# Moving each expert's short tile from last to third of five in a mixture-of-experts kernel, with two-tile transpositions and an earlier count

## The chip, the cores and the metric

The kernel runs on one core of a Trainium2 chip. Its engines are TensorE (PE in the profile; its weight loads are PEld), VectorE (DVE), ScalarE (ACT), GpSimd (POOL) and SyncE (SP). The metric is the device time of one execution in microseconds, lower is better. The core's span is the time from the first to the last instruction of the program in a profiled execution.

## The reference

`x` is 8 x 256 tokens of 1024 values. A gated feed-forward layer with a low-rank correction, chosen per batch, gives `cond`; a router then sends every token to two of eight experts, and the mean of the two experts' outputs is added to `x`.

```python
def cond_layer(x):                              # F = 2752, rank 16
    gate = x @ W_gate.T + 0.5 * (x @ A_gate[i].T) @ B_gate[i].T
    up   = x @ W_up.T   + 0.5 * (x @ A_up[i].T)   @ B_up[i].T
    act  = silu(gate) * up
    return act @ W_down.T + 0.5 * (act @ A_down[i].T) @ B_down[i].T

def experts(c):                                 # E = 8, TOP_K = 2, D = H = 1024
    logits = c @ W_gate + b_gate
    _, top = top_k(logits, 2)
    y_all = relu(einsum('bsd,edh->bseh', c, W_e) + b_e)
    return take_along_axis(y_all, top[..., None], axis=2).mean(axis=2)

out = x + experts(cond_layer(x))
```

All of it is in float32.

## The kernel before

The first 1600 us compute `cond` with Strassen's scheme in two halves of 1024 tokens, write its rows to DRAM (`cond_rows`) and work out the routing. The change does not touch that part.

The rest handles the experts. 4096 token rows go to 8 experts, about 512 to each, and are cut into tiles of 128 rows. An expert has `NJ` = 5 tile positions, 40 in all (`NPOS`). Tiles 0 to 3 of an expert are nearly always full; tile 4 holds what exceeds 512 rows, so it has few rows or none. Expert 0 is shifted by one, because one of its tiles is done ahead (`pre_tile`, L1259): its position 3 is the short one, and its position `NJ - 1` is a leftover tile that is empty in this run. Here four short tiles are empty (the leftover and position 3 of expert 0, experts 1 and 6), and five have at most 32 rows (experts 2, 3, 4, 5 and 7). Five positions of expert 0 and of experts 1 to 7 are 40; 31 of them are full tiles.

A tile goes through these steps:

- `load_rows` (L1437) gathers the tile's 128 rows of `cond_rows` with an indirect DMA on POOL's queue, `AHEAD` = 4 tiles ahead in `SEQ`.
- `rows_transposed` (L1124) transposes them: two halves of four TensorE transposes each, each half in a PSUM bank of its own (`ps_g`), copied out by ScalarE (L1133). Four sums of these blocks (`s`) follow on VectorE, or on POOL for expert 0's two short tiles.
- `one_tile` (L1497) claims four PSUM banks (`tile_banks`, L1208) and branches on the row count (L1501, L1508, L1511): more than 64 rows take `whole` (Strassen, L1153: 28 products, 56 matmul records, 14 pairs that run side by side in two halves of the array, each pair 0.86 us), 33 to 64 and 1 to 32 take `plain` (L1459) with fewer rows, and none takes `empty_tile`, which only writes 64 KB to spare rows. All engines go through the branches. `add_rows` (L1211) adds the result's rows to `out` with an indirect DMA on POOL's queue.
- In `strassen`, the first product in bank `px` is read by VectorE (`u`, L1188) before the eleventh pair may add to that bank; `py`, `pz`, `pw` and then `px` are evicted at the end (L1190 to L1199), each whole tile ending with `z<-z,v`.

PSUM has 8 banks, all from the pool of L89. The planner of the framework hands them out: a whole or a short tile takes four, a transposed tile two.

The order of the tiles is `SEQ` (L1526). `BEHIND` (L1529 to L1533) lists which tiles are transposed behind which: behind tile 0 of an expert its tile 2, behind tile 1 its tile 3, behind tile 2 the next expert's tile 0 and its own tile 4, behind tile 4 the next expert's tile 1. The weights of the next expert are loaded on SP's queue in tile 0's place (four loads of 1 MB, L1091), and the four sums of weight blocks (`ws`, L1103, `sums_e`) run on VectorE behind tiles 1 (two), 2 and 3, the sum of biases (L1205, L1206) behind tile 3. The framework's planner keeps the order of each engine's instructions close to the order in which the program writes them, with what isn't ready by its own reckoning put later; everything inside a branch is one unit that nothing is mixed into.

After the last tile `over`, `ntile`, `novf` and `nov` (L1601 to L1613) count the tiles beyond five per expert (none here), `value` (L1487) loads the count into a register on every engine, and L1615 branches on it.

Of the kernel before, what the change touches and what calls it, by code (L numbers as in the profile page):

```python
# [9 lines left out]
I32 = mybir.dt.int32  # L10
# [3 lines left out]
ALU = mybir.AluOpType  # L14
AX = mybir.AxisListType
P = 128
# [4 lines left out]
E, TOP_K = 8, 2  # L21
T = B * S
# [24 lines left out]
C_THR = C_END + E  # L47
# [6 lines left out]
NJ = 5  # L54
NPOS = E * NJ
# [10 lines left out]
def tile_lora_glu_then_moe(ctx: ExitStack, tc: tile.TileContext, a: dict, out: bass.AP):  # L66
# [11 lines left out]
    nc = tc.nc  # L78

    const = ctx.enter_context(tc.tile_pool(name="const", bufs=1))  # L80
# [10 lines left out]
    def behind(ins, others):  # L91

        for o in others:
            tc.add_manual_dep(
                ins.ins,
                o.ins.name,
                mybir.DependencyInfo(mybir.DependencyClass.NoSync, mybir.DependencyReason.DATA),
                reason="this goes first",
            )
# [4 lines left out]
    add, sub = ALU.add, ALU.subtract  # L104
# [94 lines left out]
    ctab = const.tile([P, C_ALL], F32, name="ctab")  # L199
# [61 lines left out]
    def load_lora_gu(h):  # L261
        lora[h, "raw"] = lp.tile([P, H], F32, tag="raw", name=f"raw_gu{h}")
        return gather(lora[h, "raw"], a["A_gu"], rows["gu", h])
# [615 lines left out]
    cnt = const.tile([P, 2, E], F32, name="cnt")  # L879
# [3 lines left out]
    def small(shape, name, dt=F32, tag=None):  # L883
        return const.tile(shape, dt, tag=tag or name, name=name)
# [195 lines left out]
    def load_e(e, first=()):  # L1080

        m = e % 2
        if m == 0 and W[0] is None:
            W[0] = {
                (kh, nh): xp.tile([P, WB], F32, tag=f"x1_{kh}{nh}", name=f"we_{kh}{nh}")
                for nh in range(2)
                for kh in range(2)
            }
            WS[0] = [xp.tile([P, WB], F32, tag=f"xt1_{i}", name=f"ws_{i}") for i in (1, 2, 3)]
        loads = [  # L1090
            nc.sync.dma_start(W[m][kh, nh], a[f"W_e{kh}{nh}"][e * P : (e + 1) * P, :])  # L1091
            for kh, nh in ((0, 0), (0, 1), (1, 1), (1, 0))
        ]
        for ins in loads:
            behind(ins, first)
        return loads

    def sums_e(e, which, first=()):
        b11, b12, b21, b22 = (W[e % 2][kh, nh] for kh in range(2) for nh in range(2))
        t = WS[e % 2]  # L1100
        for i in which:
            x, y = ((b12, b11), (b22, t[0]), (b22, b12), (b21, t[1]))[i]
            ins = nc.vector.tensor_tensor(t[i], x, y, sub)  # L1103
            behind(ins, first)
            if e == 1:
                issued.append(ins)
# [3 lines left out]
    adds, earlier = [], []  # L1110
# [92 lines left out]
    def sum_bias(dst, b, first=()):  # L1203
        b0, b1 = b[:, :NB], b[:, NB:]
        behind(nc.vector.tensor_copy(dst[lo], b0[lo]), first)  # L1205
        behind(nc.vector.tensor_tensor(dst[hi], b0[hi], b1[hi], sub), first)  # L1206
# [75 lines left out]
    ins = load_lora_gu(0)  # L1282
# [21 lines left out]
    for h in range(2):  # L1304
# [8 lines left out]
        if h == 0:  # L1313
            first = [latest["v"]]
# [30 lines left out]
    for n, (h, g) in enumerate(steps):  # L1345
# [4 lines left out]
        for i in range(NI):  # L1350
            if n and out_rows:

                lo_, hi_, at = out_rows.pop(0)
                ins = nc.gpsimd.dma_start(out[at : at + hi_ - lo_, :], a["x"][lo_:hi_, :])
# [77 lines left out]
    def load_bias(e):  # L1432
        nc.sync.dma_start(braw[e % 2], a["b_e"][e : e + 1, :].partition_broadcast(P))
# [3 lines left out]
    def load_rows(i, col):  # L1437
        gathered[i] = gp.tile([P, H], F32, tag="g", name=f"g{i}")
        issued.append(indirect(gathered[i], cond_rows, col))
# [47 lines left out]
    def value(table, i):  # L1487
        return nc.values_load(  # L1488
            table[:1, i : i + 1], skip_runtime_bounds_check_because="worked out on VectorE"
        )  # L1490
# [6 lines left out]
    def one_tile(i, n, at, gT, A):  # L1497

        m, col = i // NJ % 2, columns(i)[1]
        done, banks = [], tile_banks(i)  # L1500
        with tc.If(n > at + HALF) as full:  # L1501
            done.append(add_rows(whole(i, A, m, banks), P, col))
        if at < 0:
            with full.Else():
                done.append(empty_tile(i))
            return done
        with full.Else():
            with tc.If(n > at + HALF // 2) as half:  # L1508
                done.append(add_rows(plain(i, gT, m, 2, banks), HALF, col))
            with half.Else():  # L1510
                with tc.If(n > at) as some:  # L1511
                    done.append(add_rows(plain(i, gT, m, 4, banks), HALF // 2, col))
                with some.Else():
                    done.append(empty_tile(i))
        return done

    def columns(i):


        if i == NJ - 1:  # L1520
            return gidx1, sidx1
        c = i + 1 if i < NJ else i
        return gidx[:, c : c + 1], sidx[:, c : c + 1]


    SEQ = [0, 1, NJ - 1] + list(range(2, NJ - 1)) + list(range(NJ, NPOS))  # L1526


    BEHIND = {0: (NJ - 1, 2), 1: (3,), NJ - 1: (NJ,), 2: (NJ + 1,), 3: ()}  # L1529
    late = []  # L1530
    for i in range(NJ, NPOS):
        j = i % NJ
        BEHIND[i] = ((i + 2,), (i + 2,), (i + 3, i + 2), (), (i + 2,))[j]  # L1533
    AHEAD = 4
    for i in SEQ[:3]:
        load_rows(i, columns(i)[0])
    load_bias(0)
    first = list(issued)
# [3 lines left out]
    for e in range(E):  # L1542
        n = value(cnti, e)
        for j in range(NJ):
            i = SEQ[e * NJ + j]
            if j + e == 0:
                load_rows(SEQ[3], columns(SEQ[3])[0])
            if e * NJ + j + AHEAD < NPOS:
                k = SEQ[e * NJ + j + AHEAD]
                load_rows(k, columns(k)[0])  # L1550
            if i == NJ - 1:
                tile_done = one_tile(i, value(cnti, E), -HALF, *ready.pop(i))
            else:
                tile_done = one_tile(i, n, (i % NJ + (e == 0)) * P, *ready.pop(i))
            adds += tile_done
            issued.clear()
            if e == 0 and j == 4:
                sums_e(1, (1, 3), tile_done)
                sum_bias(bsum[1], braw[1], tile_done)
            while late:  # L1560
                late.pop()()
            if e + 1 < E:

                if j == 0:
                    for ins in load_e(e + 1):
                        if e == 0:
                            for row in first:
                                tc.add_manual_dep(
                                    ins.ins,
                                    row.ins.name,  # L1570
                                    mybir.DependencyInfo(
                                        mybir.DependencyClass.Sync, mybir.DependencyReason.DATA
                                    ),
                                    reason="rows first",
                                )
                            issued.append(ins)
                    load_bias(e + 1)
                elif e:
                    sums_e(e + 1, ((), (0, 2), (1,), (3,), ())[j], tile_done)
            for k in BEHIND[i]:  # L1580
                if k < NPOS:
                    short = k in (3, NJ - 1)
                    ready[k] = transposed(
                        k, op=pop if short else vop, late=late if k == NJ + 1 else None
                    )
            if e == 0 and j == 2:
                sums_e(1, (0, 2), tile_done)
            if 0 < e < E - 1 and j == 3:
                sum_bias(bsum[(e + 1) % 2], braw[(e + 1) % 2], tile_done)
        earlier[:] = adds  # L1590
        adds.clear()


    NTT = T // P
    op = ctx.enter_context(tc.tile_pool(name="over", bufs=1))

    def osmall(shape, name, dt=F32):
        return op.tile(shape, dt, tag=name, name=name)

    over = osmall([P, E, NTT], "over")  # L1600
    ins = nc.vector.tensor_tensor(  # L1601
        over,
        cnt[:, 1].unsqueeze(2).to_broadcast([P, E, NTT]),
        ctab[:, C_THR : C_THR + NTT].unsqueeze(1).to_broadcast([P, E, NTT]),
        ALU.is_gt,
    )
    behind(ins, earlier)
    ntile = osmall([P, E], "ntile")
    nc.vector.tensor_reduce(ntile, over, AX.X, add)
    novf = osmall([P, 1], "novf")  # L1610
    nc.vector.tensor_reduce(novf, ntile, AX.X, add)
    nov = const.tile([P, 1], I32, name="nov")
    nc.vector.tensor_copy(nov, novf)  # L1613
    nover = value(nov, 0)
    with tc.If(nover > 0):  # L1615
        before = osmall([P, E, E], "before")
        vop(
# [219 lines left out]
```

## Time and profile before

| | us |
|---|---|
| median of 3 runs | 2098.92 |
| lowest and highest run | 2092.86, 2099.81 |
| the profiled execution's own time | 2096.54 |
| its span, first to last instruction | 2094.7 |
| TensorE busy | 2052.9 (98%) |
| VectorE busy | 1246.9 (60%) |
| GpSimd busy | 1057.9 (51%) |
| ScalarE busy | 250.4 (12%) |
| mean granted TensorE clock | 0.995 of full speed |

Rows of the timeline give start and duration in us, engine, line, operation, names of the tiles written and read, shapes, and in brackets how long the engine was idle before and what ended that. `PEq`, `DVEq` and the like are the engines' sequencers, which run branches, register loads and waits. A row of the windows view gives a stretch of time, its length, each engine's busy time and number of instructions, the granted clock, and the share and rate of the DMA engines.

The experts' stage in us from the span's start: the tile done ahead until 1613, expert 0 from 1616.7, experts 1 to 7 from 1664.2, 1723.3, 1785.2, 1847.3, 1907.3, 1968.6 and 2026.9; the last tile's matmuls end at 2084.1.

### The profile page before, as it was taken

Reading aid. Unit: us, or ns where it says so; the run is one execution under the profiler, and the core shown is the slowest. Engines: PE = TensorE matmul, PEld = TensorE weight load, DVE = VectorE, ACT = ScalarE, POOL = GpSimd, SP = SyncE. Lnnn points to the kernel's source line nnn. Section 1 sums busy time; section 2 is a strip of 40 time slices with the busy share of each in tenths; the row PEclk is TensorE's granted clock in tenths of the full one; section 3 lists DMA queues with packets and bytes.
Section 4 is the critical chain, followed back from the end, with each engine's and each line's share of the span. In section 5 each row is a group of like instructions: output and inputs, shape, how many; then the busy total and the mean of one; then the engine's idle time right before and its main releaser. Section 6 shows DMA issues by size and latency. Waiting matters only on the chain. (4 is left out here: it accounts for less than half of the span.)

```text
span 2094.7 us, 20377 instructions
## 1 busy us (share of the span) xinstructions
PE 2052.9 (98%) x6864; PEld 867.2 (41%) x6864; DVE 1246.9 (60%) x1734; ACT 250.4 (12%) x450; POOL 1057.9 (51%) x976
## 2 busy tenths in 40 slices
PE   8999999999999999999999999999999999999997
PEld 3444444444444444444444444444444433333332
DVE  6757466565656656566545443654556676666674
ACT  1001011110101011110100001100002111212111
POOL 2447676675667757665355553565542432322221
PEclk9999999999999999999999999999999999999999
DMA  7675676757667575686433335222324754565632
GB/s 313 246 263 191 241 254 217 261 174 271 209 228 292 182 260 192 230 286 200 144 125 126 126 118 176 101 95 87 118 83 157 222 160 133 159 181 166 182 75 46
DMA packets 108234, 381.73 MB, mean 182 GB/s; under 512 B 12656, under 2 KB 21136, under 8 KB 100304
## 3 DMA queue, kind: packets, MB, share of 16 engines
q1 hardware_dynamic: 81280, 297.98, 40.2%
q0 software_dynamic: 13952, 58.53, 10.6%
q10 hardware_dynamic: 12848, 23.22, 3.1%
q8 instruction: 90, 1.47, 0.3%
q14 instruction: 64, 0.52, 0.1%
HBM read 318.47 MB, written 72.74 MB: 187 GB/s over the span
## 5 line engine op out<-in xcount | busy, mean ns | idle before, releaser
L335 PE MATMUL ps_u<-x,wi 128*128 128x512 f32 x880 | 396.1, 593 | 0.5 <-DMA x<-in_xq 0.5
L113 POOL TENSOR_TENSOR cond<-cond,u_d 128x512 f32<-128x512 f32 x120 | 150.2, 1267 | 231.5 <-DVE u_d L108 231.5
L335 PEld LDWEIGHTS ps_u<-x,wi 128*128 128x128 f32 x880 | 166.9, 190 | 212.4 <-issue 202.0
L335 PE MATMUL ps_u<-x,w 128*128 128x512 f32 x520 | 241.7, 599 | 0.3 <-DMA x<-xs 0.2
L1215 POOL DMA_INDIRECT out<-y,sidx x36 | 74.9, 2080 | 325.8 <-ACT y L1122 295.5
L1174 PE MATMUL ps_x<-we,gT 128*64 128x512 f32 x496 | 231.7, 611 | 1.7 <-DVE z L108 1.1
L108 DVE TENSOR_TENSOR u_u<-ps_u,u_u 128x512 f32<-128x512 f32 x210 | 144.9, 690 | 141.1 <-PE ps_u L335 135.6
L108 DVE TENSOR_TENSOR cond<-ps_d,cond 128x512 f32<-128x512 f32 x160 | 103.8, 686 | 115.2 <-POOL cond L113 40.8
L1174 PE MATMUL ps_z<-ws,s 128*64 128x512 f32 x372 | 157.7, 592 | 0.0
L335 PEld LDWEIGHTS ps_u<-x,w 128*128 128x128 f32 x520 | 96.0, 190 | 134.0 <-issue 126.5
L335 PE MATMUL ps_d<-a,wd 128*128 128x512 f32 x320 | 151.3, 595 | 0.0
L108 DVE TENSOR_TENSOR u_d<-ps_d,u_d 128x512 f32<-128x512 f32 x120 | 82.9, 691 | 113.5 <-PE ps_d L335 111.5
L335 PE MATMUL ps_d<-at,wd 128*128 128x512 f32 x320 | 150.4, 592 | 0.0
L335 PE MATMUL ps_d<-at,wds 128*128 128x512 f32 x320 | 145.1, 596 | 0.0
L1174 PE MATMUL ps_y<-ws,s 128*64 128x512 f32 x248 | 119.8, 628 | 0.0
L113 POOL TENSOR_TENSOR acc<-acc,u_u 128x512 f32<-128x512 f32 x60 | 74.3, 1267 | 86.3 <-DVE u_u L108 74.2
L335 PE MATMUL ps_u<-xt,wi 128*128 128x512 f32 x240 | 112.8, 592 | 0.0
L1174 PE MATMUL ps_x<-ws,gT 128*64 128x512 f32 x248 | 111.5, 592 | 0.0
L1174 PE MATMUL ps_y<-we,s 128*64 128x512 f32 x248 | 111.5, 592 | 0.0
L1174 PEld LDWEIGHTS ps_x<-we,gT 128*64 128x64 f32 x496 | 66.2, 140 | 103.7 <-issue 102.9
L108 DVE TENSOR_TENSOR u<-ps_z,u 64x512 f32<-64x512 f32 x62 | 42.6, 687 | 103.0 <-PE ps_w L1174 85.8
L113 POOL TENSOR_TENSOR wi<-w 128x256 f32<-128x256 f32 x100 | 85.4, 874 | 26.3 <-PE ps_u L335 18.3
(273 smaller groups left out, 3135.2 us busy)
## 6 DMA issues: line engine op xcount, KB each, us to landing
x<-xs SPq DMA_DIRECT2D x240, 512.0 KB, 4.6
x<-in_xq SPq DMA_DIRECT2D x74, 512.0 KB, 4.8
we<-in_W_e SPq DMA_DIRECT2D x32, 1024.0 KB, 10.2
a<-act SPq DMA_DIRECT2D x42, 512.0 KB, 4.7
w<-in_W SPq DMA_DIRECT2D x20, 1024.0 KB, 9.2
wd<-in_W_d SPq DMA_DIRECT2D x40, 512.0 KB, 3.2
xs<-xi SPq DMA_DIRECT2D x24, 512.0 KB, 2.9
out<-in_x POOLq DMA_DIRECT2D x22, 512.0 KB, 4.0
```

The source lines that it names most:

```text
L108: ins = nc.vector.tensor_tensor(dst, x, y, op)
L113: ins = nc.gpsimd.tensor_tensor(dst, x, y, op)
L335: ins = nc.tensor.matmul(ps, A(ai, j), X(xi, j), start=(j == 0 and bank is None), stop=(j == n - 1 and stop), skip_group_check=True,)
L1174: ins = nc.tensor.matmul(dst, w[:, k, :], x[:, k * NB : (k + 1) * NB], start=start, stop=stop, skip_group_check=True,)
L1215: added = nc.gpsimd.indirect_dma_start(out=out, out_offset=bass.IndirectOffsetOnAxis(ap=col[:n], axis=0), in_=y[:n], in_offset=None, compu ...
```

## The change

Four things change.

- `SEQ` puts position 4 third for every expert, as it was for expert 0 alone: 0, 1, 4, 2, 3.
- `BEHIND` follows. Behind the first tile of an expert the third and fourth in the new order are transposed (tile 4 and tile 2), behind the second the fifth (tile 3), behind the fourth (tile 2) the first two tiles of the next expert (tiles 0 and 1), and behind tile 4 and the fifth nothing. Expert 0's leftover tile no longer has a transposition behind it; the next expert's first two tiles are both transposed behind its tile 2.
- The sums of weight blocks move with it: two behind the third place (the short tile, index `j` = 2) and two behind the fourth (tile 2), none behind the second. The sum of biases stays at index 3, which is now tile 2.
- The count of further tiles and its load into registers move from the end of the program to just behind expert 7's tile 1, before the transposition there; the branch on it stays at the end.

```diff
-    SEQ = [0, 1, NJ - 1] + list(range(2, NJ - 1)) + list(range(NJ, NPOS))
+    SEQ = [e * NJ + j for e in range(E) for j in (0, 1, NJ - 1, *range(2, NJ - 1))]

-    BEHIND = {0: (NJ - 1, 2), 1: (3,), NJ - 1: (NJ,), 2: (NJ + 1,), 3: ()}
+    BEHIND = {0: (NJ - 1, 2), 1: (3,), NJ - 1: (), 2: (NJ, NJ + 1), 3: ()}
+    for n in range(NJ, NPOS):
+        j = n % NJ
+        ahead_ = ((2, 3), (4,), (), (5, 6), ())[j]
+        BEHIND[SEQ[n]] = [SEQ[n - j + m] for m in ahead_ if n - j + m < NPOS]
     late = []
-    for i in range(NJ, NPOS):
-        j = i % NJ
-        BEHIND[i] = ((i + 2,), (i + 2,), (i + 3, i + 2), (), (i + 2,))[j]
+    NTT = T // P
+
+    def tiles_over(first):
+        over = small([P, E, NTT], "over")
+        ins = nc.vector.tensor_tensor(
+            over,
+            cnt[:, 1].unsqueeze(2).to_broadcast([P, E, NTT]),
+            ctab[:, C_THR : C_THR + NTT].unsqueeze(1).to_broadcast([P, E, NTT]),
+            ALU.is_gt,
+        )
+        behind(ins, first)
+        ntile, novf, nov = small([P, E], "ntile"), small([P, 1], "novf"), small([P, 1], "nov", I32)
+        nc.vector.tensor_reduce(ntile, over, AX.X, add)
+        nc.vector.tensor_reduce(novf, ntile, AX.X, add)
+        nc.vector.tensor_copy(nov, novf)
+        return ntile, value(nov, 0)
...
                 elif e:
-                    sums_e(e + 1, ((), (0, 2), (1,), (3,), ())[j], tile_done)
+                    sums_e(e + 1, ((), (), (0, 2), (1, 3), ())[j], tile_done)
+            if (e, j) == (E - 1, 1):
+                ntile, nover = tiles_over(tile_done)
             for k in BEHIND[i]:
...
-    over = osmall([P, E, NTT], "over")
...
-    nover = value(nov, 0)
     with tc.If(nover > 0):
```

More of the change, by code (lines that the diff above doesn't have):

```diff
@@ L1591, in tile_lora_glu_then_moe @@
         adds.clear()
-    NTT = T // P
     op = ctx.enter_context(tc.tile_pool(name="over", bufs=1))
@@ L1598, in osmall @@
         return op.tile(shape, dt, tag=name, name=name)
-    over = osmall([P, E, NTT], "over")
[L1601 to L1613, printed above, removed]
-    nover = value(nov, 0)
     with tc.If(nover > 0):
```

## The prediction

> I forecast **2106 us, slower by about 0.35%**. An expert's tiles 0 to 3 are called whole; tile 4 is the short one, which runs few rows or is empty.
>
> **What bounds the kernel now.** First the page, for the bound.
>
> ```profile
> PE 2052.9 (98%) x6864; PEld 867.2 (41%) x6864; DVE 1246.9 (60%) x1734; ACT 250.4 (12%) x450; POOL 1057.9 (51%) x976
> ```
>
> TensorE is busy 98% of the span, so a change is worth what it does to TensorE's idle stretches. The change touches only the experts' tiles, from about 1613 us on. There TensorE's timeline around the first empty short tile (expert 1) reads:
>
> ```profile
> 1717.57 1.02 PE L1174 MATMUL ps_x<-ws,gT 128*64 128x512 f32 x2
> 1720.14 0.63 PE L1130 MATMUL ps_g<-ident,g 128*128 128x128 f32 x4 [1.56 <-DVE z L108]
> 1722.57 0.63 PE L1130 MATMUL ps_g<-ident,g 128*128 128x128 f32 x4 [1.80 <-DVEq L1511]
> ```
>
> Brackets give the idle time before a row and who ended it. The next transposition needs two PSUM banks. Tile 3 and the short tile have claimed four each of the eight (L1208, whether used or not). Its first half waits until VectorE has emptied tile 3, its second until VectorE has left the short tile (L1511). Where the short tile has rows, only the second half waits (expert 2):
>
> ```profile
> 1784.39 0.63 PE L1130 MATMUL ps_g<-ident,g 128*128 128x128 f32 x4 [1.57 <-DVE z L108]
> ```
>
> Now expert 2's two transpositions in a row, behind tile 2:
>
> ```profile
> 1763.58 1.97 PE L1130 MATMUL ps_g<-ident,g 128*128 128x128 f32 x16
> ...
> 1764.53 0.69 DVE L108 TENSOR_TENSOR z<-z,v 64x512 f32<-64x512 f32 x1
> ...
> 1765.47 1.07 PE L1174 MATMUL ps_x<-we,gT 128*64 128x512 f32 x2
> 1765.79 1.54 ACT L1133 COPY gT<-ps_g 128x512 f32<-128x512 f32 x3
> ...
> 1766.41 0.13 PEld L1174 LDWEIGHTS ps_y<-ws,s 128*64 128x64 f32 x1 [0.75 <-ACT gT L1133]
> ```
>
> Here tile 2 and four halves claim all eight banks, and the next tile's second product (ps_y) starts 0.94 us behind its first, when ScalarE's first copy has freed a bank. The other whole tiles last 12.2 us to the next transposition; this one lasts 13.17. Last, expert 0, whose empty tile stands third already:
>
> ```profile
> 1643.87 1.09 PE L1130 MATMUL ps_g<-ident,g 128*128 128x128 f32 x8
> ...
> 1647.07 1.09 PE L1130 MATMUL ps_g<-ident,g 128*128 128x128 f32 x8 [2.11 <-ACTq L1501]
> ```
>
> It is the nearest picture of what every expert becomes.
>
> **The change part by part.** "+" is slower.
>
> *The short tile leaves the end.* Idle time removed: expert 1 3.36, expert 6 3.35, experts 2 to 5 1.57 each (6.28), and ahead of the short tiles 0.29 (expert 3) and 1.09 (expert 5): 14.4 us. The clock record also has 3.41 us at half speed from 1723.7, 1785.1 and 2027.5, behind the short tiles of experts 1, 2 and 6; each costs half of that, together 5.1. The windows view shows the first:
>
> ```profile
> 1718.00:1728.00 10.00, 6.52 (x24) 2.61 (x24) 6.40 (x10) 2.44 (x4) 4.49 (x3) 0.83 0.83 270
> ```
>
> Granted clock 0.83 is 3.41 of 10 us at half speed. The Trainium skill (TensorE: Matmul & The Clock Gate, "Why this matters for your kernels") lets the clock fall only for idle gaps above about 3 us. No gap here reaches that; by the rule nothing is gained, by the row 5.1. I take the row: about 1.8 us of idleness inside one 3.41 us window was enough. Sum -19.5.
>
> *Two transpositions behind tile 0.* Tile 0 now follows tile 3 directly, so those two hold all eight banks. By the rows of 1720.14 and 1722.57 the first half takes a bank of the older tile (free) and the second one of the tile just ended. VectorE's last row of a whole tile ends 1.65 us after its matmuls (1765.22 against 1763.58); the second half could start at 0.55, so 1.1 is lost, 1.2 with the restart. Bounds: 0, if other banks come first, and 1.2; near the upper, because the 0.94 of the other pair lies there. Seven experts, +8.4. Behind tile 2, which follows the short tile directly, the same wait takes the place of 0.94: +0.26 for six, +1.6.
>
> *The short tile third.* With rows it follows a transposition and has old banks. But TensorE must branch past the code of the whole tile, and some branches are slow:
>
> ```profile
> L1501 PEldq COMPARE_BRANCH  x71: 65/184/5422, 1616.4 to 2076.3; - x71
> ```
>
> Seven of the eight short tiles with a full choice of branches meet one of 1.7 to 5.4 us. The Trainium skill (Runtime: NRT & Kernel Launch, "Instruction fetch mechanics") says that a taken branch to code outside the fetched pages waits for a DMA; it speaks against this move. By itself it would charge the whole stall, 3.7 on the average of those seven. By the trace only what exceeds the lead of TensorE's sequencer is lost: 4.9 us ahead at the end of tile 3 (1835.5 against 1840.4), where 4.63 cost 0.29; behind a single transposition it is 3.7 ahead (1687.7 against 1691.4). With stalls of the same sizes the mean loss is 0.73, bounds 0 and 2.3. Experts 2 to 5: +2.9. The rule alone would make it +13.
>
> Empty (experts 1 and 6): tile 2's first bank is one that ScalarE's copy behind tile 1 must free, as in expert 0: 2.1, lower bound 1.10 (expert 0's second empty tile). The clock then falls with a chance of 0.6, 1.0 on average. +6.2.
>
> *Expert 0.* The third place keeps its 2.1. Tile 2's matmuls now fill the rest of that clock window; the 1.7 of the drop at 1648.6 becomes 1.0. One more transposition's sums (four of 0.42) go ahead of the two weight sums before the next tile, whose first eviction was 0.8 late already: +0.8. With +0.3 at the pair: +0.4.
>
> *Count of further tiles.* The chain moves ahead of expert 7's short tile. Its end today:
>
> ```profile
> 2086.10 0.29 DVE L1601 TENSOR_TENSOR over<-cnt,ctab 128x128 f32<-128x128 f32 x1
> ...
> 2086.79 1.32 POOL L1215 DMA_INDIRECT out<-y,sidx  x1 [2.37 <-ACT y L1122]
> 2086.95 0.15 DVE L1613 CAST nov<-novf 128x1 int32<-128x1 f32 x1
> ```
>
> Four VectorE operations take 1.0, five register loads about 0.3 each in parallel. Today they cost nothing: the last rows land at 2090.6, and the end waits for that. Moved, TensorE's load waits for VectorE: 1.65 for tile 1's eviction, 1.0 and 0.36, so 3.0 after tile 1. Behind it are queued the branches and then the short tile's matmuls, which could start at 1.1 and now start about 4.1. The lead is gone, so a slow branch (3.5 in this place today) shows in full, and the clock may fall. Bounds: 0 if the planner puts the load behind the short tile, and 8. I take 5.5, nearest to the chain with a stall.
>
> *The end.* A whole tile now ends the program. Its rows need 5.95 us from issue to the last packet (2069.68 to 2075.63), 32 rows 3.8 (2086.79 to 2090.6); evictions are equal. +1.95. Tile 3 of expert 7 follows tile 2 with no transposition between, and may wait for it up to 1.65: +0.8.
>
> *At nothing.* The weight sums (2.29 each) move to places three and four. From expert 2 on, two of them already run behind tile 2 with eight row sums and end before the next tile needs its first eviction; if three gathered there, VectorE would be 1.5 late per expert. A possible bias sum (1.1) behind them: +0.3. Gathers stay four places ahead on POOL's queue, one issue of 1.0 each; the tightest, behind tile 1's add, lands about 11 us after tile 1 and is needed after 15. SP's weight loads start at tile 3's end and have 27 us.
>
> Sum: -19.5 + 8.4 + 1.6 + 2.9 + 6.2 + 0.4 + 5.5 + 1.95 + 0.8 + 0.3 = +8.6. The profiled execution took 2096.5 (span 2094.7 and 1.8 around it): 2105.1. The runs' median, 2098.9, stands 2.4 higher, as one or two more clock drops would; I add half: **2106**.
>
> **Rivals.** *The count waits for nobody:* its load lands behind the short tile. For it: loads follow the planner's order; against: the chain is written first. -5.5: 2100.5, within 0.3% of the median. *The pairs find free banks:* no second-half waits (10.0): 2096, no change. For it: four banks of tile 3 are long empty; against: the 1722.57 row. *Banks rotate past every conflict:* one mechanism with the sign turned. Besides those 10.0, the 0.94 of the old pairs (6.6) and the idle times of the two empty tiles with their clock (4 of 6.2) go as well, because all pairs take banks emptied a tile ago: about 2085. It decides from about 13 us of the 21. *VectorE collects three weight sums behind tile 2:* 1.5 for six experts, 2115; against: the loads land early.
>
> **How the numbers follow.** Forecast 0.45, count hidden 0.20, free banks 0.18, all banks 0.12, VectorE 0.05. Slower by over 0.3% (about what a measurement of this kernel can tell from no change, 6.3 us) 0.50, within 0.38, faster 0.12. The range 2093 to 2115 leaves out the faster case and some of the last; the forecast alone spans 2101 to 2111.
>
> **What would show it.** Right: no gap ahead of an expert's first tile; behind tile 0, four transposes, a gap near 1.1 that VectorE ends, then twelve; gaps near 2.1 behind tile 1 in experts 1 and 6; in expert 7 TensorE idle 3 us or more behind tile 1. Wrong: tile 0's pair running in 1.97 without a gap and the next tile in 12.2, or the count's load standing behind the short tile.

## The result, and the profile after

The changed kernel takes **2100.18 us** (median of 14 runs, 2096.74 to 2103.1); the kernel before took 2096.73 on the same chip (14 runs). The ratio is 1.0016 with a 95% interval of 1.0009 to 1.0022: slower by 0.16%, less than the 0.3% that I had set as the bound of a change. The forecast was 2106, slower by 0.35%. The profiled execution has a span of 2098.6 us and took 2100.4; against the 2096.5 of before that is 3.9 more, where my sum had 8.6.

TensorE's line of the page answers to the first one shown of before.

```profile
PE 2046.8 (98%) x6864; PEld 858.8 (41%) x6864; DVE 1243.5 (59%) x1734; ACT 250.0 (12%) x450; POOL 1052.0 (50%) x976
```

It is 6 us less busy in a span 4 us longer. The clock record has three half-speed stretches in the stage in place of four, and what was a wait inside a busy row before (the 0.94 of ps_y, while ps_x ran on) is now idle time. Where TensorE stood still, its timeline shows (start, duration, line, operation, in brackets the idle time before it and who ended it). The first three rows are expert 0, the next five expert 3, the last two expert 7.

```profile
1661.71 0.66 PE L1130 MATMUL ps_g<-ident,g 128*128 128x128 f32 x4
1663.57 1.50 PE L1130 MATMUL ps_g<-ident,g 128*128 128x128 f32 x12 [1.21 <-DVE z L108]
1668.91 0.61 PE L1174 MATMUL ps_x<-we,gT 128*64 128x512 f32 x1 [3.83 <-issue]
...
1800.84 0.66 PE L1130 MATMUL ps_g<-ident,g 128*128 128x128 f32 x4
1802.71 1.50 PE L1130 MATMUL ps_g<-ident,g 128*128 128x128 f32 x12 [1.21 <-DVE z L108]
...
1833.09 1.09 PE L1130 MATMUL ps_g<-ident,g 128*128 128x128 f32 x8
1835.06 1.06 PE L1130 MATMUL ps_g<-ident,g 128*128 128x128 f32 x8 [0.88 <-DVE z L108]
...
1845.21 0.64 PE L1174 MATMUL ps_x<-we,gT 128*64 128x512 f32 x1 [0.34 <-DVE u L108]
...
2056.57 1.09 PE L1130 MATMUL ps_g<-ident,g 128*128 128x128 f32 x8
2057.60 0.64 PE L1473 MATMUL ps_x<-we,gT 128*32 128x256 f32 x8
```

1802.71 is what the forecast described: four transposes behind tile 0, a wait of 1.21 us that VectorE ends, then twelve. 1835.06 is the wait in the pair behind tile 2, and 1845.21 a second one inside the tile that follows, which I had not put on the path. 1668.91 is the largest loss of the stage, behind expert 0's second empty place. 2057.60 is what did *not* happen: expert 7's short tile starts at the end of the transposition, although the count had been put in between. The register loads of the count, by line, tell why:

```profile
L1488 SPq TENSOR_LOAD <-nov x1: 273/273/273, 2059.3 to 2059.3; - x1
L1488 PEldq TENSOR_LOAD <-nov x1: 312/312/312, 2081.2 to 2081.2; - x1
L1488 DVEq TENSOR_LOAD <-nov x1: 315/315/315, 2086.6 to 2086.6; - x1
```

SyncE loads the count at 2059.3, behind expert 7's tile 1. TensorE's load stands at 2081.2, behind the branches of the last tile: the planner put it where the value is used.

A ledger of the stage, from the starts of tiles and transpositions in both traces. An undisturbed whole tile takes 12.17 us to the next start, one transposition 1.02, a pair 1.90, a short tile 3.59; what exceeds that is loss. "+" is slower.

| step of the forecast | forecast | measured |
|---|---|---|
| short tile leaves the end (idle time and half clock of before) | -19.5 | -21.8 |
| pair behind tile 0 (six of 1.40, and 0.82 in expert 1's tile 1) | +8.4 | +9.2 |
| pair behind tile 2 (1.53 for 0.93 before, six times) | +1.6 | +3.6 |
| short tile third, with rows | +2.9 | 0 |
| short tile third, empty (2.18; 2.30 and 1.70 of clock) | +6.2 | +6.2 |
| expert 0 up to and with expert 1's tile 0 (12.6 for 7.3) | +0.4 | +5.3 |
| count of further tiles | +5.5 | 0 |
| the end | +1.95 | +2.5 |
| expert 7's tile 3, directly behind tile 2 | +0.8 | -0.2 |
| weight and bias sums | +0.3 | in the third row |
| fewer seams (a pair for two singles, tiles in direct succession) | none | -1.3 |
| the untouched part before 1614.5 | none | +0.5 |
| sum | +8.6 | +4.0 (span +3.9) |

### The profile page after: what moved, and what is told of

Its sections match the earlier page's. It is cut to its first block, busy times and chain, and to the rows that moved or that the text cites. A ratio compares the mean times of both kernels' runs of the same rounds, so it can differ in the third digit from the quotient of the medians.

```text
span 2098.6 us, 20373 instructions
## 1 busy us (share of the span) xinstructions
PE 2046.8 (98%) x6864; PEld 858.8 (41%) x6864; DVE 1243.5 (59%) x1734; ACT 250.0 (12%) x450; POOL 1052.0 (50%) x976
## 3 DMA queue, kind: packets, MB, share of 16 engines
q0 software_dynamic: 13952, 58.53, 10.8%
## 5 line engine op out<-in xcount | busy, mean ns | idle before, releaser
L1174 PE MATMUL ps_z<-ws,s 128*64 128x512 f32 x372 | 162.2, 592 | 0.0
```

The source lines that it names most:

```text
L1174: ins = nc.tensor.matmul(dst, w[:, k, :], x[:, k * NB : (k + 1) * NB], start=start, stop=stop, skip_group_check=True,)
```

## The experiments

Each ratio is against runs of the kernel before on the same chip, taken together with it; "above" or "below the changed kernel" means the difference from its ratio of 1.0016. Each ratio is known to between 0.001 and 0.002 either way, so a difference of about 0.12% between two of them is at the edge of what can be told.

**The count alone.** The kernel before, with only the count moved.

```diff
+            if (e, j) == (E - 1, 1):
+                ntile, nover = tiles_over(tile_done)
             for k in BEHIND[i]:
...
-    over = osmall([P, E, NTT], "over")
...
-    nover = value(nov, 0)
     with tc.If(nover > 0):
```

> The kernel before with one part of the change: the count of further tiles and its register loads stand behind expert 7's tile 1; order, transpositions and weight sums are the old ones. The prediction's step (TensorE's load waits for VectorE behind tile 1 and what is queued behind it stands still): TensorE idle about 3 us behind expert 7's tile 1, time 3 to 5.5 us above the kernel before. The rival (the planner puts TensorE's load where its value is used, at the end): no idle stretch behind that tile, time within 1 us of the kernel before, TensorE's load in the last two tiles.

Measured: 2095.46 us, ratio 0.9996 (0.9985 to 1.0006). Behind expert 7's tile 1 there is no idle stretch, and TensorE's load is again far down, behind the branches of the last tile:

```profile
L1488 SPq TENSOR_LOAD <-nov x1: 272/272/272, 2054.8 to 2054.8; - x1
L1488 PEldq TENSOR_LOAD <-nov x1: 313/313/313, 2080.9 to 2080.9; - x1
```

Moving the count costs nothing and brings nothing. The step of 5.5 us falls.

**The count where every engine must have it.** Was the price wrong, or only the place? A branch that is not taken uses the value at once.

```diff
                 ntile, nover = tiles_over(tile_done)
+                with tc.If(nover > 0):
+                    ordered(nc.gpsimd.dma_start(out[T : T + P, :P], ident))
```

> The changed kernel with a branch on the count right behind its load in expert 7 (not taken here; its body would write 64 KB to spare rows), so that every engine must have the value before it goes on to the short tile. It measures the price that the prediction put on the count. By the prediction: TensorE idle about 3 us or a little more behind expert 7's tile 1, perhaps a half-speed stretch and a slow branch, 5 us above the changed kernel (4 to 8). Rival (the value is ready early enough, the transposition hides it): under 1.5 us of idle time there and no change in time.

Measured: 2104.09 us, ratio 1.0039 (1.0025 to 1.0053), 0.23% or 4.8 us above the changed kernel. TensorE's timeline, VectorE's, the load and a windows row (length, busy times, then granted clock, DMA share and rate):

```profile
2055.22 1.09 PE L1130 MATMUL ps_g<-ident,g 128*128 128x128 f32 x8
2059.43 5.35 PE L1473 MATMUL ps_x<-we,gT 128*32 128x256 f32 x64 [3.12 <-DVE s L108]
```

```profile
2057.75 0.15 DVE L1550 CAST nov<-novf 128x1 int32<-128x1 f32 x1
```

```profile
L1488 PEldq TENSOR_LOAD <-nov x1: 316/316/316, 2057.9 to 2057.9; - x1
```

```profile
2058.00:2068.00 10.00, 8.57 (x80) 4.51 (x82) 3.38 (x8) 2.15 (x6) 2.08 (x2) 0.83 0.36 55
```

The count is done 1.6 us after the transposition's end, the load follows at once, the short tile starts after 3.1 us of idleness and takes 5.35 us in place of 3.66, because the clock fell (0.83 of full speed in that window). 3.1 and 1.7 are the 4.8, and in the profiles the stretch from this transposition to the last matmul is 33.7 us for 28.9. The row names VectorE's `s` sums, which the short tile does not read; TensorE's sequencer goes through the load and five branches, none above 0.24 us, until 2059.3. So the wait on record was right and the 5.5 near, but made up otherwise: a half-speed stretch came, a slow branch did not. The price belongs to a use of the value in that place, which the change doesn't have.

**Expert 0's transpositions as before.**

```diff
-    BEHIND = {0: (NJ - 1, 2), 1: (3,), NJ - 1: (), 2: (NJ, NJ + 1), 3: ()}
+    BEHIND = {0: (NJ - 1, 2), 1: (3,), NJ - 1: (NJ,), 2: (NJ + 1,), 3: ()}
```

> The changed kernel with expert 0's transpositions where they were before (one tile behind its empty third place, one behind its tile 2); the rest as changed. Theory (behind tile 2 the pair's second tile holds TensorE's sequencer at a wait for VectorE, so that the branches of the empty tile behind it start 1.2 us before the work runs out instead of 3, and their 3.4 us show): the gap of 3.83 us ahead of expert 1's tile 0 falls to about 1.1, the half-speed stretch behind it and the pair's 1.21 go, so expert 0 takes 47.5 us from its tile 0 to expert 1's in place of 51.4 and the time falls by 3 to 4 us. Rival (a branch to that code costs its 2.7 us wherever the transpositions stand): the gap stays at 3 us or more and the time within 1.5 us of the changed kernel.

Measured: 2096.69 us, ratio 1.0001 (0.9991 to 1.0011), 0.15% or 3.1 us below the changed kernel. Expert 0 takes 47.35 us from its tile 0 to expert 1's, for 51.44. TensorE's timeline there, and the slow branch (count, shortest/median/longest in ns, start) in this kernel:

```profile
1662.34 1.09 PE L1130 MATMUL ps_g<-ident,g 128*128 128x128 f32 x8
1664.43 0.61 PE L1174 MATMUL ps_x<-we,gT 128*64 128x512 f32 x1 [1.00 <-DVE z L108]
```

```profile
L1511 PEldq COMPARE_BRANCH  x1: 2967/2967/2967, 1660.5 to 1660.5; - x1
```

and the same branch in the changed kernel:

```profile
L1511 PEldq COMPARE_BRANCH  x1: 2718/2718/2718, 1664.4 to 1664.4; - x1
```

The branch is slow in both, 2.97 and 2.72 us. TensorE's sequencer works ahead of the engine, and a branch costs nothing as long as that lead covers it. In the old arrangement it starts at 1660.5, before the last transposition begins (1662.34), and is over by its end. In the new one the transposition's second half waits for VectorE until 1663.57, the branches queued behind that wait run from 1663.6, and the slow one from 1664.4; TensorE is out of work at 1665.08, the register load behind the branch ends at 1668.6, and 3.83 us are lost. A wait in the work took the cover from a branch. In this profile part of the gain is hidden: the branches of expert 1's empty tile were slower than in the changed kernel's profile (3.7 and 3.2 for 2.1 and 2.9) and cost 2.5 us more with the clock.

**Weight sums as before.**

```diff
-                    sums_e(e + 1, ((), (), (0, 2), (1, 3), ())[j], tile_done)
+                    sums_e(e + 1, ((), (0, 2), (1,), (3,), ())[j], tile_done)
```

> The changed kernel with the four weight sums where they were (two behind tile 1, one behind the short tile, one behind tile 2); the rest as changed. Theory (three weight sums of 2.29 us stand in a row behind tile 2 and make VectorE late for tile 3's first eviction): the gaps of 0.34 us inside tile 3 go, tile 3 takes 12.1 to 12.2 us to the next tile in place of 12.63, the gap of 0.88 in the pair ahead of it stays; six experts, 2 to 3 us below the changed kernel. Rival (the row sums or the pair's late copies are what makes VectorE late, or the planner gathers the sums again): 12.6 us and no change in time.

Measured: 2096.06 us, ratio 1.0004 (0.9994 to 1.0014), 0.12% or 2.5 us below the changed kernel, which the times alone can hardly tell; the timeline can. VectorE in the changed kernel, between the end of expert 3's tile 2 and the first eviction of its tile 3:

```profile
1834.12 0.69 DVE L108 TENSOR_TENSOR z<-z,v 64x512 f32<-64x512 f32 x1
1834.84 2.29 DVE L1103 TENSOR_TENSOR ws<-we,we 128x2048 f32<-128x2048 f32 x1
1837.05 2.28 DVE L1103 TENSOR_TENSOR ws<-we,ws 128x2048 f32<-128x2048 f32 x1
...
1839.59 2.28 DVE L1103 TENSOR_TENSOR ws<-we,ws 128x2048 f32<-128x2048 f32 x1
...
1844.47 0.68 DVE L108 TENSOR_TENSOR u<-ps_x,b 64x512 f32<-64x512 f32 x1
```

Three weight sums stand in a row; with eight row sums and a part of the bias sum they keep VectorE busy until 1844.47, when TensorE already waits. With the old arrangement the pair keeps its 0.88 and the tile behind it runs without the second wait:

```profile
1830.38 1.06 PE L1130 MATMUL ps_g<-ident,g 128*128 128x128 f32 x8 [0.88 <-DVE z L108]
```

The tile takes 12.07 us to the next start, for 12.63. So the smallest rival of the forecast ("VectorE collects three weight sums behind tile 2") did come about, at a third of its price: 0.5 per expert, not 1.5.

**Banks handed out by hand.** The compiled program of the changed kernel says which banks are used around the beginning of expert 2 (x, y, z, w are the four banks of a tile, x is emptied last):

```text
expert 1 tile 3:           x7 y1 z4 w0
expert 2 tile 0:           x3 y2 z6 w5
pair behind it, 4 halves:  7 3 0 1
```

The second half gets bank 3, x of the tile just ended, while 0 and 1 have long been free and are given to the third and fourth. Expert 1's tile 0 has x7 y3 z6 w4, and the halves behind it got 0, 5, 1 and 2, none of its banks; there the pair ran without a gap:

```profile
1682.91 1.97 PE L1130 MATMUL ps_g<-ident,g 128*128 128x128 f32 x16
```

The forecast had read the wait as "those two hold all eight banks". The run with named banks tells the two apart: it closes the pool at the start of the experts' part and opens one in which every bank is named.

```diff
+    cps.close()
+    fixed["pool"] = ctx.enter_context(tc.tile_pool(name="psf", bufs=1, space=PSUM))
...
     def tile_banks(i):
-        return [psum(f"ps_{n}{i}") for n in "xyzw"]
+        m = SEQ.index(i) % 2 if fixed else 0
+        return [psum(f"ps_{n}{i}", f"{n}{m}") for n in "xyzw"]
...
+            m = (e * NJ + j + 1) % 2
+            fixed["half"] = [f"{r}{n}" for n in ((m, 1 - m) if len(BEHIND[i]) > 1 else (1 - m,)) for r in "zw"]
             for k in BEHIND[i]:
```

> The changed kernel with its PSUM banks handed out by hand in the experts' part: tiles take two sets of four in turn, and a transposed half takes a bank of a tile's third or fourth product, never of its first two. Theory (the wait of 1.21 us behind tile 0 comes from the choice of the bank that the tile just ended empties last, while three banks of the older tile are free): no gap in the pair behind tile 0 (seven of 1.21), none in the pair behind tile 2, and the gaps of 2.1 us at the three empty third places fall to 1 or less. VectorE's three weight sums behind tile 2 start when that tile's eviction ends, so the 0.88 us saved in that pair come back as waits for tile 3's first eviction (about 1.3 us there). Sum: 8.5 for the first pairs, 4 for the empty places, 2 to 3 for clock: 12 to 15 us below the changed kernel. Rival (all eight banks are taken, so some wait is there whichever bank is chosen): gaps near 1 us stay behind tile 0 and the time within 4 us of the changed kernel.

Measured: 2085.19 us, ratio 0.9951 (0.9933 to 0.9968), 13.6 us below the changed kernel. TensorE, expert 3:

```profile
1796.19 1.97 PE L1134 MATMUL ps_g<-ident,g 128*128 128x128 f32 x16
...
1827.21 1.97 PE L1134 MATMUL ps_g<-ident,g 128*128 128x128 f32 x16
1839.32 0.64 PE L1178 MATMUL ps_x<-we,gT 128*64 128x512 f32 x1 [1.41 <-DVE u L112]
```

Both pairs run in 1.97 without a gap, so nothing needed to wait there. (The change of pools has its price: 3.35 us of idleness ahead of the stage's first transposition, for 1.53.) And as expected, the 0.88 saved in the second pair came back as a longer wait for VectorE, 1.41 for 0.34, since VectorE's three weight sums start no earlier. One step missed: of the three empty third places, expert 0's and expert 6's fell to 0.70 and 0.81 us as expected, but expert 1's rose to 2.89. And behind expert 0 a third transposition came ahead of expert 1's tile 0, with waits of 1.87 and 1.33 us between the three.

**The old order with the same banks.** If all that the short tile cost at the end was a bad bank too, the move would have been needless. The diff is the one above on the kernel before, except that a pair's two tiles take the two sets of banks in the other order, and the transpositions keep the order in which they are written.

```diff
+            fixed["half"] = [f"{r}{n}" for n in (1 - m, m) for r in "zw"]
...
-                nc.tensor.transpose(
+                ins = nc.tensor.transpose(
...
+                    behind(ins, fixed.get("last", []))
+                    fixed["last"] = [ins]
```

> The kernel before, with nothing of the change, but PSUM banks handed out by hand in the experts' part as in the run with fixed banks (tiles take two sets of four in turn, a transposed half takes a bank of a tile's third or fourth product) and the transpositions kept in the order in which they are written. Theory (what the old order lost at its short tiles was the choice of banks, not the order): the gaps of 1.57 us behind experts 2 to 5 and of 1.56 and 1.80 behind experts 1 and 6 go, tile 3 takes 12.2 us in place of 13.1 after the pair, and the half-speed stretches go with them: 14.4 + 6 x 0.94 + 5 = 25 us, about 2072 to 2076. Rival (a short tile at the end leaves a wait for VectorE whichever banks are chosen, so that the move is needed for the gain): the gaps behind the short tiles stay at 1 us or more, 2085 or above.

Measured: 2089.97 us, ratio 0.9968 (0.9957 to 0.998). In time it is what the rival said (2085 or above); of the gaps neither was right throughout. Where the short tile has rows, its wait shrinks from 1.57 to 0.76; where it is empty, it grows to 4.06:

```profile
1788.52 1.07 PE L1134 MATMUL ps_g<-ident,g 128*128 128x128 f32 x8 [0.76 <-issue]
...
2021.70 1.94 PE L1134 MATMUL ps_g<-ident,g 128*128 128x128 f32 x8 [4.06 <-DVEq L1522]
```

```profile
2018.53 0.69 DVE L112 TENSOR_TENSOR z<-z,v 64x512 f32<-64x512 f32 x1
2019.25 2.29 DVE L1107 TENSOR_TENSOR ws<-we,ws 128x2048 f32<-128x2048 f32 x1
2021.69 0.42 DVE L1212 COPY bsum<-b 64x512 f32<-64x512 f32 x1 [0.15 <-DVEq L1522]
```

TensorE may not use the banks of the empty tile before VectorE has left its branch, and VectorE does tile 3's eviction and a weight sum first. I had expected that wait to go with the choice of banks. With these banks it hangs on when VectorE reaches and leaves the branch; banks of tile 3 in place of the empty tile's were not tried.

**The old order without that weight sum.**

```diff
-                    sums_e(e + 1, ((), (0, 2), (1,), (3,), ())[j], tile_done)
+                    sums_e(e + 1, ((), (0, 2), (1, 3), (), ())[j], tile_done)
```

> The old order with fixed banks, and its last weight sum moved from behind tile 3 to behind tile 2, so that VectorE has no weight sum of 2.29 us to do between tile 3 and the empty short tile's branch. It sets the old order against the new one with banks and weight sums at their best in both. Theory (the 4.06 us behind tile 3 of experts 1 and 6 are tile 3's eviction, 1.65, and that weight sum): they fall to about 1.8 and the half-speed stretches shrink, some 6 to 9 us below 2090, 2081 to 2084; then the new order is worth 3 to 6 us with good banks, the rest of the 11.6 us between the two runs with fixed banks was the weight sums. Rival (the empty branch itself holds TensorE, by a slow branch of 3.4 to 3.7 us): 4 us stay and the time is 2088 to 2090; the new order is worth all of the 11.6.

Measured: 2087.46 us, ratio 0.9961 (0.9948 to 0.9975). The 4.06 fall to 2.89, less than expected, because the bias sum (1.1 us) takes the weight sum's place ahead of the branch:

```profile
2016.46 1.89 PE L1134 MATMUL ps_g<-ident,g 128*128 128x128 f32 x8 [2.89 <-DVEq L1522]
```

The fall of 1.17 is what VectorE's queue ahead of the branch lost, 2.29 for 1.1. The gain in time over the run before is not clear of its scatter.

**The new order with banks and weight sums.** The bank rule and the fixed order of transpositions of the last two runs on the changed kernel, and the weight sums spread.

```diff
-                    sums_e(e + 1, ((), (), (0, 2), (1, 3), ())[j], tile_done)
+                    sums_e(e + 1, ((), (0,), (2, 1), (3,), ())[j], tile_done)
```

> The changed kernel with its banks handed out by hand in the same way, the transpositions kept in the order in which they are written, and the four weight sums spread: one behind tile 1, two behind the short tile, one behind tile 2. Theory (with fixed banks alone the waits of 1.41 us for VectorE inside tile 3 were the weight sums gathered behind tile 2): those six waits go, 1.4 each, and the two gaps of 1.9 and 1.3 us between transpositions behind expert 0 go too, so about 10 us below the run with fixed banks alone (2085.2): 2074 to 2078. If the kernel before with fixed banks is as fast or faster, the new order earns nothing by itself. Rival (something other than the weight sums makes VectorE late in tile 3): 1.4 us stay inside tile 3, 2082 to 2085.

Measured: **2078.36 us, ratio 0.9917 (0.9904 to 0.993)**, 17 us faster than the kernel before and the best of all. TensorE, expert 0 and expert 3:

```profile
1658.86 1.97 PE L1134 MATMUL ps_g<-ident,g 128*128 128x128 f32 x16
1664.91 1.08 PE L1181 MATMUL ps_x<-we,gT 128*64 128x512 f32 x1 [4.09 <-DVEq L1522]
...
1823.70 1.97 PE L1134 MATMUL ps_g<-ident,g 128*128 128x128 f32 x16
1834.69 0.64 PE L1181 MATMUL ps_x<-we,gT 128*64 128x512 f32 x1 [0.29 <-DVE u L112]
```

The wait for VectorE inside tile 3 falls from 1.41 to 0.29, which is why I read it as the weight sums'. The order of a pair's sets and of the transpositions changed with them, so this run alone does not isolate it; the run that moved only the sums back points the same way (0.34 to none).

The gap behind expert 0's second empty place did not go, although the pair ahead of it now runs without one:

```profile
L1522 PEldq COMPARE_BRANCH  x1: 3017/3017/3017, 1660.4 to 1660.4; - x1
```

The sequencer began with that tile's branches at 1658.88, as the pair began, and came out of them and of the load at 1664.5; the pair's work ended at 1660.82. So the pair of transpositions need not stand idle for the cover to be too short. Why the branches began no earlier I did not isolate.

By the same measure as in the ledger, 14.9 us are lost in the stage, for 34.9 in the kernel before and 36.7 in the changed one. Against the old order with banks and sums set (0.9961) the new one is worth 0.44%, 9 us. The old order's bias sum was left ahead of its empty branches; at 1.1 us in two experts I estimate that some 2 of the 9 us could be had there too, which no run tried.

**Expert 7 in the old order.**

```diff
+    SEQ[-NJ:] = range(NPOS - NJ, NPOS)
...
+        if n >= NPOS - NJ:
+            ahead_ = ((2,), (3,), (4,), (), ())[j]
```

> The changed kernel with expert 7 alone in the old order (tiles 0, 1, 2, 3, short) and one transposition behind each of its first three tiles; the count stays behind its tile 1. Theory (a whole tile's 128 rows at the end take longer from the last matmul to the end of the span, 13.2 us, than the short tile's 32 rows, 10.6): the tail falls to 10.6 us, the pair's gap of 1.21 in expert 7 stays in one form or another and the short tile may wait up to 1.1 us for a bank, so 1 to 3 us below the changed kernel. Rival (what comes after the last rows sets the end): the tail stays at 13 us and the time is that of the changed kernel.

Measured: 2099.14 us, ratio 1.0014 (1.0008 to 1.0021): no clear change from the changed kernel. From the last matmul to the end of the span it is 12.8 us, not 10.6. The short tile's rows do land 3.8 us after their issue,

```profile
DMA to landing us min/median/max: 3.8/5.2/6.7
```

that is at 2090.2, but POOL stays at its last waits until 2092.9. What it waited for I could not read from the trace. With a short tile at the end the tail was 10.6 us in the kernel before, 10.8 in the run with the count alone and 12.8 here, so the last tile's size does not set it by itself; whether it has a part is not shown.

## Why the prediction was wrong, by its own steps

- *Short tile leaves the end*, -19.5: right, and 2.3 larger. I took the idle times alone; each broke a transposition in two, so the next tile started up to 0.4 later than the gap says.
- *Pairs behind tile 0*, +8.4: right in place, size and who ends it (1.21, forecast 1.2) in six of the seven experts; the seventh lost 0.82 inside its tile 1. Its reason was wrong: what makes the second half wait is not that two tiles hold all banks, but that it is given the bank emptied last while others are free. With other banks the wait is gone. The rival "the pairs find free banks" had the fact right that four banks are long empty; the planner just doesn't choose them. Why it ranks x so early I only suppose: it is the one bank that the branches for few rows use as well.
- *Pair behind tile 2*, +1.6: measured +3.6. The wait in the pair was sized right (1.07 over an undisturbed pair, forecast 1.2); the second one, for VectorE (0.46 over an undisturbed tile), had been left to a rival with a chance of 0.05 and "the loads land early" against it. I checked whether the weights are there, and not in which order the planner lines the sums up.
- *Short tile third, with rows*, +2.9: **failed**. In experts 2 to 5 and 7 the slowest branches in this place took 1.31, 1.35 and 1.06 us, two experts had none above 0.7, all under the 3.7 of TensorE's lead. I had carried over stalls of 1.7 to 5.4 from the fifth place. The mean loss of 0.73 does not follow from the figures beside it either: those seven stalls against a lead of 3.7 give 0.44, at most 1.7.
- *Empty third places*, +6.2: right, 2.18 in expert 1 and 4.00 with the clock in expert 6. I had put a chance of 0.6 on the clock in each; that one of two met it and the sum fits to a tenth is luck.
- *Expert 0*, +0.4: **failed**, +5.3. The lead that covers a branch was computed for single transpositions and never for the pair behind tile 2, where 1.5 us of it are left (1663.6 to 1665.08). The step "+0.3 at the pair" priced the wait and not what is queued behind it. Of the 5.3, 4.1 are the longer gap ahead of expert 1's tile 0 and 1.0 the half-speed stretch that follows it; the 0.7 that I expected to save at the first empty place did not come.
- *Count*, +5.5: **failed**, 0, the largest error and the one that turned no clear change into a forecast of slower. The forecast gave 0 as the lower bound "if the planner puts the load behind the short tile" and named this as a sign of being wrong. Where the value is really used, the wait came as described and the price was near (4.8), with a half-speed stretch in place of the slow branch.
- *The end*, +1.95: +2.5 in the profiles; its cause stays open. (The two durations that the forecast shows, 5.95 and 3.8, differ by 2.15, not 1.95.)
- *Half of the median's offset*, +1.2: wrong. It took the median of three runs as the kernel's; fourteen gave 2096.7, close to the profiled execution's own 2096.5.

So the count and the branches made the sum 8.4 too high, the larger gain at the end and the seams another 3.6, and expert 0 and VectorE 6.9 too low. The rival "the count waits for nobody" gave 2100.5, and 2100.18 was measured; that it fits so closely is partly chance, since the other errors nearly cancel.

## What to carry to other kernels

- The price of a moved operation is paid where its result is *used*. Ask first which instruction consumes it and whether the framework will keep the load at the place where you wrote it.
- When a tile waits for a buffer, look up which buffer it was given and which ones stood free. A good change of order (here worth 9 us when both orders have named banks) can be spent entirely on allocation, and naming the buffers by hand brought it back here.
- A wait of 1 us in an engine's work can also hold up its sequencer, so that branches and register loads behind it lose their cover (here 1.21 us of waiting left 1.5 us of lead, and 3.83 were lost); and an eviction made earlier gains nothing if the engine that evicts is the next one late.

## What the runs showed of the hardware that I had not expected

- Idle gaps of nearly the same length do different things to the clock. The windows view of the changed kernel around the gaps of experts 6 and 1:

```profile
1995.00:2005.00 10.00, 7.77 (x32) 2.75 (x30) 6.76 (x11) 2.22 (x4) 3.21 (x3) 0.83 0.43 84
1697.00:1707.00 10.00, 7.89 (x40) 2.92 (x38) 6.28 (x9) 2.22 (x4) 3.20 (x3) 1.00 0.47 97
```

  Expert 6 (2.23 us idle) loses 1.70 us to the clock, expert 1 (2.11 us) nothing, and expert 0's first empty place (2.11 us) again 1.70. The length of a gap between 2.1 and 2.3 us does not decide it. All three are below the 3 us that the Trainium skill (TensorE: Matmul & The Clock Gate, "Why this matters for your kernels") gives as the idle gap to stay under.

  Where a gap lies may decide it. By the clock record the half-speed stretches of this trace begin at 1649.08, 1669.56 and 2000.65, which is 6 and 97 times 3.413 us apart, so they keep to a grid of that step. The gaps of expert 6 (1997.30 to 1999.53) and expert 0 (1645.73 to 1647.84) lie wholly inside one step, and the stretch begins at that step's end; the grid cuts expert 1's (1698.89 to 1701.00) into 1.38 and 0.72. In the run with the weight sums as before the same gap of expert 0 is cut into 0.92 and 1.19 and loses nothing, and with fixed banks neither does one of 2.89 us, cut into 1.58 and 1.31. This is read off the traces; no run moved a gap to test it.
- One and the same branch, behind expert 0's second empty place, took 3.11 us in the kernel before, 2.72 in the changed one, 2.97 and 4.43 in two of the experiments. In the last of these, the count alone, where the code around it is that of before, it outran its lead and the gap there was 2.48 us in place of 1.10. A slow branch that is covered today is not safe to leave uncosted.
